# Wider store rows, and loads on a queue of their own, in a kernel that is bound by its DMA engines

## The chip, the cores and the metric

One core of one Trainium2 chip runs the kernel. The time is device microseconds of one execution; most executions of one kernel lie within 0.3% of its median, and a few of the kernel before were up to 0.8% above it (773.18 us). Every kernel that is compared by time was run in rounds beside the kernel before, on the same chip, and once with a profile; the experiments were made on three chips, so steps between them go by the ratio to the kernel before. The ratios use runs of the fast state alone.

## The reference, cut to what matters

For each of the 496 pairs (i, j) of 32 fields, a vector of 128 numbers is multiplied by the pair's own 128 x 128 matrix, and the result by another field's vector, all in float32 and for 1024 rows:

```python
v_i = inputs[:, I_IDX, :]                              # (1024, 496, 128)
v_j = inputs[:, J_IDX, :]
transformed = jnp.einsum('bpd,ped->bpe', v_i, W)       # W is (496, 128, 128)
return transformed * v_j                               # 260 MB of output
```

Output 260 MB, inputs and weights 49 MB: much traffic for the arithmetic.

## The kernel before

All inputs stay in SBUF (32 tiles of 4 KB a partition). Weights come in chunks of eight pairs, each as two half loads of 64 partitions, and are split by ScalarE and GpSimd into parts that take TensorE less time (three products that start 0.227 us apart, where the native float32 product of half a pair takes 0.858 us). ScalarE scales the first sum in PSUM, TensorE adds the correction, VectorE multiplies by the other field into an output tile, and SyncE stores the tile when its two pairs are done. SyncE issues nearly all loads too, in program order, on its one queue.

```python
OG = 2                                                       # pairs of one store
rpool = ctx.enter_context(tc.tile_pool(name="wr", bufs=3))   # raw weights
opool = ctx.enter_context(tc.tile_pool(name="o", bufs=4))    # output
...
def load_w(c, half, splits=(0, WL)):                         # WL = 8 pairs
    if c not in w_raw:
        w_raw[c] = rpool.tile([P, WL, P], F32, tag="w", name=f"w_{c}")
    for a, b in zip(splits, splits[1:]):
        nc.sync.dma_start(out=w_raw[c][half::2, a:b, :], in_=wt[c, half, :, a:b, :])
...
def second(u):                                               # u: half a pair
    ...                                                      # third matmul
    nc.vector.tensor_tensor(ots[g][:, k, s], po.pop(u), x_sb[j][:, s], ALU.mult)
    if q >= NQ - 2:
        nc.sync.dma_start(out=out[g, :, k, s], in_=ots[g][:, k, s])
    elif k == OG - 1 and h == 1:
        nc.sync.dma_start(out=out[g], in_=ots[g])
...
for u in range(2 * NQ + LAG):
    q = u // 2
    if u % (2 * WL) == 4 and (q // WL + 2) * WL < NQ:
        load_w(q // WL + 2, 1)
    if u % (2 * WL) == 12 and (q // WL + 3) * WL < NQ:
        load_w(q // WL + 3, 0)
    ...                                                      # load_x, first(u), second(u - LAG), splits
```

Of the kernel before, what the change touches and what calls it, by code (L numbers as in the profile page):

```python
# [7 lines left out]
F32 = mybir.dt.float32  # L8
# [3 lines left out]
P = 128  # L12
NF = 32
NQ = NF * (NF - 1) // 2
BT = 1024
HB = 512
WC = 2
WL = 8
OG = 2
EPS = 2.0**-12  # L20
NATIVE = 5
SHARED = 10
XDLAG = 10
LAG = 3
XLEAD = 5


def _pairs():

    return [(i, j) for i in range(NF - 2, -1, -1) for j in range(i + 1, NF)]  # L30


@with_exitstack
def kernel(
    ctx: ExitStack,
    tc: tile.TileContext,
    xt: bass.AP,
    wt: bass.AP,
    out: bass.AP,
):  # L40
















    nc = tc.nc
    pairs = _pairs()
    nchunk = NQ // WC

    xpool = ctx.enter_context(tc.tile_pool(name="x", bufs=1))
    spool = ctx.enter_context(tc.tile_pool(name="xs", bufs=2))
    rpool = ctx.enter_context(tc.tile_pool(name="wr", bufs=3))
    wpool = ctx.enter_context(tc.tile_pool(name="ws", bufs=4))
    opool = ctx.enter_context(tc.tile_pool(name="o", bufs=4))
    ppool = ctx.enter_context(tc.tile_pool(name="ps", bufs=8, space=bass.MemoryType.PSUM))

    x_sb = {}

    def load_x(f, n=1, pieces=1, eng=None):  # L70

        t = xpool.tile([P, n, BT], F32, tag=f"x{f}", name=f"x_{f}")
        s = BT // pieces
        for k in range(pieces):
            (eng or nc.sync).dma_start(out=t[:, :, k * s : (k + 1) * s], in_=xt[:, f : f + n, k * s : (k + 1) * s])
        for k in range(n):
            x_sb[f + k] = t[:, k, :]

    w_raw = {}

    def load_w(c, half, splits=(0, WL)):

        if c not in w_raw:
            w_raw[c] = rpool.tile([P, WL, P], F32, tag="w", name=f"w_{c}")
        for a, b in zip(splits, splits[1:]):
            nc.sync.dma_start(out=w_raw[c][half::2, a:b, :], in_=wt[c, half, :, a:b, :])

    w_s = {}

    def split_w(c, u):  # L90

        k = c * WC % WL
        raw = w_raw[c * WC // WL][:, k : k + WC, :].rearrange("p q e -> p (q e)")
        h, l, d = [wpool.tile([P, WC * P], F32R, tag=t, name=f"{t}_{c}") for t in ("wh", "wl", "wd")]
        nc.scalar.mul(h, raw, 1.0 - 2.0**-13)  # L95
        nc.gpsimd.tensor_tensor(l, raw, h.bitcast(F32), ALU.subtract)  # L96
        nc.gpsimd.tensor_scalar(d, h.bitcast(F32), EPS, 1.0, ALU.mult, ALU.mult)  # L97
        nc.gpsimd.tensor_tensor(d, l.bitcast(F32), d.bitcast(F32), ALU.subtract)  # L98
        w_s[c] = (h, l, d)

    x_s = {}
    later = []

    def split_x(f, a, u):

        if a == 0:
            x_s[f] = [spool.tile([P, BT], F32R, tag=t, name=f"{t}_{f}") for t in ("xh", "xl", "xd")]
        s = slice(a, a + HB)
        h, l, d = [t[:, s] for t in x_s[f]]
        nc.scalar.mul(h, x_sb[f][:, s], 1.0 - 2.0**-13)  # L110
        nc.gpsimd.tensor_tensor(l, x_sb[f][:, s], h.bitcast(F32), ALU.subtract)  # L111
        nc.gpsimd.tensor_scalar(l, l.bitcast(F32), 1.0 / EPS, 1.0, ALU.mult, ALU.mult)  # L112
        if f > NF - 2 - NATIVE - SHARED:
            later.append((min(u + XDLAG, 2 * first_q[f] + LAG - 1), d, h.bitcast(F32), l.bitcast(F32)))
        else:
            nc.gpsimd.tensor_tensor(d, h.bitcast(F32), l.bitcast(F32), ALU.subtract)  # L116

    nq0 = NATIVE * (NATIVE + 1) // 2
    c0 = nq0 // WC
    first_q = {i: q for q, (i, j) in reversed(list(enumerate(pairs)))}  # L120



    todo = []
    for c in range(c0, nchunk):
        todo.append(((c - 3) * WC + 1, max(c * WC, nq0), lambda u, c=c: split_w(c, u)))
    for i in range(NF - 2 - NATIVE, -1, -1):
        for a in range(0, BT, HB):
            todo.append((first_q[i + 1] + 1 if i < NF - 3 - NATIVE else 2, first_q[i], lambda u, i=i, a=a: split_x(i, a, u)))
    todo.sort(key=lambda t: t[1])  # L130

    load_w(0, 0, (0, 1))
    load_w(0, 1, (0, 1))
    load_w(0, 0, (1, WL))
    load_w(0, 1, (1, WL))
    load_x(NF - 2, pieces=2, eng=nc.scalar)
    load_x(NF - 1, pieces=2, eng=nc.scalar)
    load_x(NF - 3)
    load_x(NF - 4)
    load_w(1, 0)  # L140
    for f in range(NF - 5, NF - 4 - XLEAD, -1):
        load_x(f)
    load_w(1, 1)
    load_w(2, 0)


    ctx.enter_context(tc.manual_schedule())
    po, ots = {}, {}


    def first(u):
        q, h = divmod(u, 2)
        i, c = pairs[q][0], q // WC
        r = slice(q % WC * P, (q % WC + 1) * P)
        s = slice(h * HB, (h + 1) * HB)
        po[u] = ppool.tile([P, HB], F32, tag="po", name=f"po_{u}")
        if q < nq0:
            nc.tensor.matmul(po[u], w_raw[q // WL][:, q % WL, :], x_sb[i][:, s], start=True, stop=True)  # L158
        else:
            for t in (0, 1):  # L160
                nc.tensor.matmul(po[u], w_s[c][t][:, r], x_s[i][t][:, s], start=t == 0, stop=t == 1)  # L161
            nc.scalar.mul(po[u], po[u], 1.0 + EPS)  # L162

    def second(u):
        q, h = divmod(u, 2)
        i, j = pairs[q]
        r = slice(q % WC * P, (q % WC + 1) * P)
        s = slice(h * HB, (h + 1) * HB)
        if q >= nq0:
            nc.tensor.matmul(  # L170
                po[u], w_s[q // WC][2][:, r], x_s[i][2][:, s], start=False, stop=True, skip_group_check=True
            )
        g, k = divmod(q, OG)
        if k == 0 and h == 0:
            ots[g] = opool.tile([P, OG, BT], F32, tag="ot", name=f"ot_{g}")
        nc.vector.tensor_tensor(ots[g][:, k, s], po.pop(u), x_sb[j][:, s], ALU.mult)  # L176
        if q >= NQ - 2:
            nc.sync.dma_start(out=out[g, :, k, s], in_=ots[g][:, k, s])
        elif k == OG - 1 and h == 1:
            nc.sync.dma_start(out=out[g], in_=ots[g])  # L180

    for u in range(2 * NQ + LAG):
        q = u // 2
        if u % (2 * WL) == 4 and (q // WL + 2) * WL < NQ:
            load_w(q // WL + 2, 1)
        if u % (2 * WL) == 12 and (q // WL + 3) * WL < NQ:
            load_w(q // WL + 3, 0)
        if u < 2 * NQ:
            i, j = pairs[q]
            if u % 2 == 0 and j == i + 1 and 0 <= i - 2 - XLEAD:  # L190
                load_x(i - 2 - XLEAD)
            first(u)
        if u >= LAG:
            second(u - LAG)
        if u % 2 == 1:
            ready = [t for t in todo if t[0] <= q]
            if ready:
                ready[0][2](u)
                todo.remove(ready[0])
        while later and later[0][0] <= u:  # L200
            nc.vector.tensor_tensor(*later.pop(0)[1:], ALU.subtract)  # L201
    assert not todo and not later
# [27 lines left out]
```

## Time and profile before

| | before |
|---|---|
| median of 3 runs | 766.5 us |
| DMA engines, main queue's share | 98.9% |
| PE / ACT / DVE / POOL busy | 93 / 83 / 82 / 78% |
| bytes, packets | 310.12 MB, 51189 |
| VectorE waiting for a store to land | 76.3 us |

The lines themselves stand in the prediction. Read the DMA digits first: with 9 in 39 of 40 slices, work on the compute engines cannot shorten the kernel, except where it makes a transfer start earlier. In all traces of this case a row of SBUF that is contiguous in HBM shows as one packet: a store of two pairs is 128 packets of 8 KB.

### The profile page before, as it was taken

How to read it: one execution, taken by the hardware profiler on the slowest of the kernel's cores; microseconds unless marked ns; L12 is line 12 of the kernel's file. 1: busy time of each engine (PE TensorE's matmuls, PEld its weight loads, DVE VectorE, ACT ScalarE, POOL GpSimd, SP SyncE). 2: the span in 40 equal slices, each digit the busy share in tenths (PEclk: the TensorE clock that was granted, in tenths of full speed). 3: DMA queues.
4: the chain of work that ended last, by engine and by line, in shares of the span. 5: the costliest groups of instructions: out<-in, count | busy, mean ns of one | idle time of the engine just before them, and what ended most of it. 6: DMA issues, size and time to landing. Idle time of an engine off the chain costs nothing.

```text
span 766.8 us, 11879 instructions
## 1 busy us (share of the span) xinstructions
PE 715.1 (93%) x2946; PEld 547.0 (71%) x2946; DVE 631.9 (82%) x1012; ACT 634.0 (83%) x1256; POOL 594.8 (78%) x863
## 2 busy tenths in 40 slices
PE   6997999999999998999999989999999999999994
PEld 2475776677767676777776768787878777777773
DVE  3878988898877787887787878888888888888895
ACT  2186988888888898888888989998989899999893
POOL 1687998879889878878788786979787879696660
PEclk9999999999999999999999999999999999999997
DMA  9999999999999999999999999999999999999997
GB/s 341 397 419 406 414 406 385 412 397 410 415 407 409 409 393 413 410 414 413 392 424 408 401 398 405 418 414 418 418 419 421 413 408 416 410 410 411 409 399 294
DMA packets 51189, 310.12 MB, mean 404 GB/s; under 512 B 6576, under 2 KB 6704, under 8 KB 19504
## 3 DMA queue, kind: packets, MB, share of 16 engines
q1 hardware_dynamic: 50544, 308.31, 98.9%
q10 hardware_dynamic: 576, 1.05, 0.4%
q8 instruction: 24, 0.39, 0.2%
q14 instruction: 45, 0.37, 0.1%
HBM read 49.28 MB, written 260.05 MB: 403 GB/s over the span
## 4 chain that ended last, share of the span: by engine, by line
DMA 45%; PE 33%; DVE 17%; issue 2%; POOL 1%; DVEq 0%; ACT 0%; ACTq 0%; POOLq 0%
DMA out_dram<-ot 44%; PE po L161 21%; DVE ot L176 16%; PE po L170 10%; PE po L158 2%; DVE xd L201 2%; DMA x<-in_xt_dram 1%; POOL xd L116 0%; POOL xl L111 0%; POOL wl L96 0%; DVEq L176 0%; POOL wd L98 0%; POOL xl L112 0%; ACT wh L95 0%; POOL wd L97 0%
## 5 line engine op out<-in xcount | busy, mean ns | idle before, releaser
L176 DVE TENSOR_TENSOR ot<-po,x 128x512 f32<-128x512 f32 x992 | 618.6, 684 | 126.0 <-DMA out_dram<-ot 76.3
L162 ACT ACTIVATE po<-po 128x512 f32<-128x512 f32 x962 | 550.5, 583 | 103.8 <-PE po L161 56.2
L161 PE MATMUL po<-xh,wh 128*128 128x512 f32 x962 | 386.8, 402 | 26.0 <-DVE ot L176 25.0
L170 PE MATMUL po<-xd,wd 128*128 128x512 f32 x962 | 377.0, 392 | 5.4 <-DVE xd L201 4.5
L161 PE MATMUL po<-xl,wl 128*128 128x512 f32 x962 | 377.8, 393 | 3.4 <-POOL wl L96 3.4
L161 PEld LDWEIGHTS po<-xh,wh 128*128 128x128 f32 x962 | 181.1, 188 | 101.5 <-DVE ot L176 63.3
L96 POOL TENSOR_TENSOR wl<-w,wh 128x256 fp32r<-128x256 f32 x241 | 180.2, 748 | 87.0 <-ACT wh L95 77.2
L170 PEld LDWEIGHTS po<-xd,wd 128*128 128x128 f32 x962 | 181.4, 189 | 46.1 <-ACT po L162 5.2
L161 PEld LDWEIGHTS po<-xl,wl 128*128 128x128 f32 x962 | 181.4, 189 | 38.2 <-POOL wl L96 5.4
L98 POOL TENSOR_TENSOR wd<-wl,wd 128x256 fp32r<-128x256 f32 x241 | 179.9, 746 | 20.1
L97 POOL TENSOR_SCALAR wd<-wh 128x256 fp32r<-128x256 f32 x241 | 99.8, 414 | 20.3
L95 ACT ACTIVATE wh<-w 128x256 fp32r<-128x256 f32 x241 | 99.2, 412 | 3.1 <-DMA w<-in_wt_dram 3.1
L111 POOL TENSOR_TENSOR xl<-x,xh 128x512 fp32r<-128x512 f32 x52 | 67.5, 1298 | 19.7 <-ACT xh L110 19.5
L116 POOL TENSOR_TENSOR xd<-xh,xl 128x512 fp32r<-128x512 f32 x32 | 41.4, 1294 | 2.7
L110 ACT ACTIVATE xh<-x 128x512 fp32r<-128x512 f32 x52 | 32.5, 629 | 11.5 <-DMA x<-in_xt_dram 11.4
L112 POOL TENSOR_SCALAR xl<-xl 128x512 fp32r<-128x512 f32 x52 | 32.6, 628 | 4.6
L158 PE MATMUL po<-x,w 128*128 128x512 f32 x60 | 30.1, 664 | 6.0 <-DMA w<-in_wt_dram 5.0
L158 PEld LDWEIGHTS po<-x,w 128*128 128x128 f32 x60 | 12.5, 212 | 22.7 <-issue 18.8
L201 DVE TENSOR_TENSOR xd<-xh,xl 128x512 fp32r<-128x512 f32 x20 | 16.5, 826 | 0.0
L110 ACT ACT_TABLE_LOAD x1 | 1.3, 1283 | 2.7 <-issue 2.7
L217 POOL MEMSET const-float32-0.0<- 128x1 f32 x1 | 0.1, 98 | 0.2 <-issue 0.2
L217 POOL MEMSET const-bfloat16-1.0<- 128x1 bf16 x1 | 0.1, 101 | 0.0
(2 smaller groups left out, 0.2 us busy)
## 6 DMA issues: line engine op xcount, KB each, us to landing
out_dram<-ot SPq DMA_DIRECT2D x247, 1024.0 KB, 8.9
w<-in_wt_dram SPq DMA_DIRECT2D x122, 256.0 KB, 9.1
x<-in_xt_dram SPq DMA_DIRECT2D x30, 512.0 KB, 8.8
x<-in_xt_dram ACTq DMA_DIRECT2D x4, 256.0 KB, 4.0
out_dram<-ot SPq DMA_DIRECT2D x4, 256.0 KB, 7.3
w<-in_wt_dram SPq DMA_DIRECT2D x2, 224.0 KB, 5.5
w<-in_wt_dram SPq DMA_DIRECT2D x2, 32.0 KB, 3.2
```

Of the source, the lines that this page charges most:

```text
L95: nc.scalar.mul(h, raw, 1.0 - 2.0**-13)
L96: nc.gpsimd.tensor_tensor(l, raw, h.bitcast(F32), ALU.subtract)
L97: nc.gpsimd.tensor_scalar(d, h.bitcast(F32), EPS, 1.0, ALU.mult, ALU.mult)
L98: nc.gpsimd.tensor_tensor(d, l.bitcast(F32), d.bitcast(F32), ALU.subtract)
L110: nc.scalar.mul(h, x_sb[f][:, s], 1.0 - 2.0**-13)
L111: nc.gpsimd.tensor_tensor(l, x_sb[f][:, s], h.bitcast(F32), ALU.subtract)
L116: nc.gpsimd.tensor_tensor(d, h.bitcast(F32), l.bitcast(F32), ALU.subtract)
L158: nc.tensor.matmul(po[u], w_raw[q // WL][:, q % WL, :], x_sb[i][:, s], start=True, stop=True)
L161: nc.tensor.matmul(po[u], w_s[c][t][:, r], x_s[i][t][:, s], start=t == 0, stop=t == 1)
L162: nc.scalar.mul(po[u], po[u], 1.0 + EPS)
L170: nc.tensor.matmul(po[u], w_s[q // WC][2][:, r], x_s[i][2][:, s], start=False, stop=True, skip_group_check=True)
L176: nc.vector.tensor_tensor(ots[g][:, k, s], po.pop(u), x_sb[j][:, s], ALU.mult)
```

## The change

Its intent: fewer and larger packets on the engines that bind (12 KB rows), and loads that do not share a queue with the stores. Four tiles of three pairs need 16 KB a partition more; one weight tile of 4 KB is given up, since beside three weight tiles four output tiles were not expected to fit. The weights are also laid out anew in HBM, so that a chunk of eight pairs comes as one load of 512 KB and not as two halves.

```diff
-OG = 2
+OG = 3
+WB = 2
+WLEAD = 6
...
-    rpool = ctx.enter_context(tc.tile_pool(name="wr", bufs=3))
+    rpool = ctx.enter_context(tc.tile_pool(name="wr", bufs=WB))
...
-    def load_w(c, half, splits=(0, WL)):
...
+    def load_w(c, splits=(0, WL), eng=nc.scalar):
+        w_raw[c] = rpool.tile([P, WL, P], F32, tag="w", name=f"w_{c}")
         for a, b in zip(splits, splits[1:]):
-            nc.sync.dma_start(out=w_raw[c][half::2, a:b, :], in_=wt[c, half, :, a:b, :])
+            eng.dma_start(out=w_raw[c][:, a:b, :], in_=wt[c, :, a:b, :])
...
+    w_at = {}
+    for c in range(WB, -(-NQ // WL)):
+        free = (c - WB + 1) * WL if (c - WB) * WL < nq0 else 0
+        w_at[max(c * WL - 3 * WC + 1 - WLEAD, free)] = c
...
+        elif g == 0 or q >= NQ - 1 - OG:
+            if h == 1:
+                nc.sync.dma_start(out=out[g, :, k], in_=ots[g][:, k])
         elif k == OG - 1 and h == 1:
             nc.sync.dma_start(out=out[g], in_=ots[g])
...
-        if u % (2 * WL) == 4 and (q // WL + 2) * WL < NQ:
-            load_w(q // WL + 2, 1)
-        if u % (2 * WL) == 12 and (q // WL + 3) * WL < NQ:
-            load_w(q // WL + 3, 0)
...
-                load_x(i - 2 - XLEAD)
+                load_x(i - 2 - XLEAD, eng=nc.scalar)
             first(u)
+            if u % 2 == 1 and q in w_at:
+                load_w(w_at[q])
```

## The prediction

> **What bounds the kernel now.** I read the page's busy shares first, then its table of 40 slices, the DMA queues and the DMA issues, then the chain of waits and the waits of each engine, and last the DMA view in two stretches of time.
>
> From the page (engine, busy us, share of the span; then DMA busy share and GB/s by slice; then queues):
> ```profile
> span 766.8 us, 11879 instructions
> PE 715.1 (93%) x2946; PEld 547.0 (71%) x2946; DVE 631.9 (82%) x1012; ACT 634.0 (83%) x1256; POOL 594.8 (78%) x863
> ...
> DMA  9999999999999999999999999999999999999997
> ...
> DMA packets 51189, 310.12 MB, mean 404 GB/s; under 512 B 6576, under 2 KB 6704, under 8 KB 19504
> ...
> q1 hardware_dynamic: 50544, 308.31, 98.9%
> ...
> DMA 45%; PE 33%; DVE 17%; issue 2%; POOL 1%; DVEq 0%; ACT 0%; ACTq 0%; POOLq 0%
> ...
> out_dram<-ot SPq DMA_DIRECT2D x247, 1024.0 KB, 8.9
> w<-in_wt_dram SPq DMA_DIRECT2D x122, 256.0 KB, 9.1
> x<-in_xt_dram SPq DMA_DIRECT2D x30, 512.0 KB, 8.8
> x<-in_xt_dram ACTq DMA_DIRECT2D x4, 256.0 KB, 4.0
> ```
> The 16 DMA engines are the bound: one queue alone fills 98.9% of their time in every slice but the last. PE's 93% looks close, but in twenty-microsecond windows where it is never idle it does about 89 matmuls, 0.225 us each; 2886 such plus 60 native ones of 0.59 us is about 685 us, an estimate of where PE would end alone.
>
> The waits of the compute engines, then those of SyncE's queue (who <- whom: us, times, longest):
> ```profile
> POOL wl L96 <- ACT wh L95: 77.2, 94, 6.2
> DVE ot L176 <- DMA out_dram<-ot: 76.3, 93, 2.6
> PEld po L161 <- DVE ot L176: 63.3, 110, 2.4
> ```
> ```profile
> SPq L180 <- DVE ot L176: 436.0, 244, 4.0
> SPq L86 <- POOL wd L98: 26.0, 26, 1.3
> SPq L86 <- POOL wd L97: 10.2, 15, 1.2
> SPq L86 <- PE po L158: 9.7, 2, 5.7
> ```
> VectorE waits 76 us for a store to land and free its tile; PE waits behind VectorE. So compute has some 10% to spare. SyncE's 436 us is only the issuer standing ready. The loads' waits on the same queue do hold up the stores behind them, some 50 us in all, but mostly about 1 us at a time, while two or three stores are still under way.
>
> The same view in a late stretch (460 to 740 us, stores and weights only) and an early one (4 to 15 us, loads only):
> ```profile
> DMA packets 17991, 115.74 MB, mean 413 GB/s; under 512 B 2337, under 2 KB 2337, under 8 KB 5409
> ...
> q1 hardware_dynamic: 17965, 115.45, 100.3%
> ```
> ```profile
> DMA packets 1330, 4.19 MB, mean 381 GB/s; under 512 B 167, under 2 KB 178, under 8 KB 1330
> ```
> Same engines, saturated both times, and fewer GB/s with small packets: there is a cost per packet. The trace's packet records (every packet has a duration and a size) give it: medians of 84 ns for 2 KB, 159 for 4 KB, 309 for 8 KB, that is 9 ns plus 75 ns for each 2 KB, and 9 ns for a completion packet of 4 B. The means are higher, 172 ns for 4 KB and 316 for 8 KB. All packets add up to 763.9 us of 16 engines.
>
> **What the Trainium skill says.** Four places, all of "DMA: Bandwidth & Descriptors".
> "Why small descriptors are slow" gives a fixed overhead of about 3 cycles a packet. At the page's 850 MHz that is 3.5 ns; the trace agrees on the kind and shows 9 ns.
> "Where 436 GB/s comes from" puts the ceiling of the 16 ports at 435 GB/s. The slope above is 2048 B in 75 ns, 27.3 B/ns, times 16 is 437 GB/s: it agrees.
> "Issuing engines are not separate DMA queues" says that DMAs of SyncE and ScalarE run on the same 16 engines and that a second issuer saves only sequencer time. So ScalarE's queue adds no bandwidth.
> "Queues, rings and completion order" says each DMA engine goes round-robin between queues, a whole packet at a time. In the first microseconds of before, where both queues are loaded, their packets do alternate roughly one for one (88 against 61 between 5 and 6 us, in the records).
>
> **The change part by part.**
>
> Wider stores. Of 496 pairs, three at the start and two near the end go out alone (5 x 128 packets of 4 KB), the last two in halves (512 packets of 2 KB, as before), the other 489 in 163 stores of 128 rows of 12 KB. Before: 31616 packets of 8 KB x 309 / 16 = 610.6 us. After: 20864 of 12 KB; the line through the medians gives 9 + 6 x 75 = 459 ns, so 598.5 us, plus 640 x 159 / 16 = 6.4 us. Saved: 5.7 us. No packet of 12 KB to or from a tile is in the trace, so 459 is an extrapolation.
>
> Fewer DMAs. Before 251 stores + 126 weight + 34 input loads = 411, times 16 = the 6576 packets under 512 B. After 172 + 63 + 34 = 269, so 4304. 2272 packets x 9 ns / 16 = 1.3 us. The weight rows themselves stay 4 KB, twice as many to a DMA: nothing more from these.
>
> The sum is 7.0 us, all on the bound. The slices with overlap read 101%, so 6.9 us of span. The excess of means over medians (7 ns on 31616 packets, 13 ns on 11648: 24 us in all) comes mostly in clusters around loads; I let it stay at about its share of time, which takes off below 0.5 us.
>
> Loads off SyncE's queue. A load waiting for its buffer no longer blocks stores. By my count over 1 us bins of the packet records, the DMA engines lost only about 4 us to dips between 20 and 750 us, so this is worth 1 to 2 us. Start (2 us until data flows) and tail (some 5 us of landing) stay.
>
> ScalarE's price. It issues 60 weight and 24 input loads more. The four it issued before took a median of 0.45 us: 84 x 0.45 = 38 us at worst, part of it under a running activation. 634 + 38 = 672 of about 758 us, 89%. It also takes over the buffer waits of SyncE's L86 rows, some 45 us, though with two tiles and a later issue most should have passed. Against the 76 us that VectorE waits for stores, this leaves compute ahead, but by less.
>
> Two weight tiles. The load is issued 6 pairs ahead of the first split: 6 x 766.8 / 496 = 9.3 us. Its 8 packets an engine, alternating with 12 KB stores, need 8 x (159 + 459) = 4.9 us, plus about 2 us of latency: 7 us, in time by about 2 us. If one is late, ScalarE stalls, while the stores in flight (three tiles of 1.5 MB, some 3.7 us each) keep the DMA engines busy. Four tiles now hold 12 pairs instead of 8, so the compute side may fall behind by more before the DMA engines see it.
>
> Together: 766.5 - 6.9 - 1.5 = 758 us; I say 757, for some gain in stalls around loads.
>
> **The rivals.**
> 1. Two queues hide load latency. The excess of 24 us clusters where loads run: 8 KB packets in the late stretch that overlap no load packet are 4 ns over the median, those that overlap 9 or more are 18 to 22 ns over. If stores fill the holes while a load waits for HBM, half of the excess goes: 745 to 748 us. For it: the clusters. Against it: the skill's sentence that the engines are shared, and that a packet's own duration need not shrink.
> 2. Alternating costs more. If the excess is paid at each turn from store to load, one-for-one alternation makes more turns than loads in a row; doubling it gives about 780 us. For it: the same clusters. Against it: the first microseconds, where both queues hold loads and the median packet is not slower; but no trace shows loads alternating with stores.
> 3. ScalarE becomes the bound. Back to back it needs 0.565 us for each product and 0.39 us for each split: 16 and 4 in eight pairs is 10.6 us, input splits add 0.5, DMA issues up to 0.65: 11.8 us where the DMA engines need 12.2. Should issues cost 1.3 us, as loads do right behind a store on SyncE, or should buffer waits recur, it passes 12.2 and the time goes to 770 or above. Against it: those 1.3 us are a queue of issues on one sequencer, and the four of ScalarE, issued beside SyncE's, took 0.38 to 0.58 us.
> 4. The gain is hidden elsewhere: nothing moves, 765 us, if 12 KB packets take more than 459 ns (468 ns would cancel all of it).
>
> **Range and chances.** The counted saving puts it at 758 to 760; rival 1 pulls to 745, rivals 2 and 3 to 770 and more. 757, 8 in 10 between 746 and 771. Faster by over 2% means below 751.2: rival 1 in good part, 0.2. Slower by over 2% means above 781.8: rivals 2 or 3 in force, 0.07. The rest, 0.73, within.
>
> **What would show it.** Packets 51189 - 10112 - 2272 = about 38800, of them 4304 under 512 B. A 12 KB median of 459 ns. DMA digits still 9 throughout and about 409 GB/s. ScalarE's queue with about 48 MB. VectorE still waiting for stores, by less than 76 us plus what the wider tiles shift. Landing of loads near 7 us. I am wrong if the DMA digits fall in mid-span (rival 3, with long waits of ScalarE on weights), or if the packet means move by more than the row size explains (rivals 1 and 2).

## The result, and the profile after

| | before | after |
|---|---|---|
| median of 6 runs each | 766.45 us | 761.4 us |
| ratio, 95% interval | | 0.9931 (0.9912 to 0.9950) |

A ratio here and below is the mean time of one kernel's fast runs over that of the kernel before in the same rounds, so it is not quite the ratio of the medians. The gain is 0.7%, some 5.3 us. Forecast were 9.5 us, with a range of 746 to 771 us.

The page of the kernel after (busy shares, DMA by slice, packets, queues, chain, issues):

```profile
span 758.7 us, 11264 instructions
PE 708.1 (93%) x2946; PEld 551.6 (73%) x2946; DVE 633.7 (84%) x1012; ACT 625.7 (82%) x1256; POOL 595.6 (78%) x863
...
DMA  9999999999999999999999999999999999999996
...
DMA packets 38800, 310.07 MB, mean 409 GB/s; under 512 B 4304, under 2 KB 4432, under 8 KB 17872
...
q1 hardware_dynamic: 26064, 264.25, 83.1%
q10 hardware_dynamic: 12672, 45.09, 16.0%
...
DMA 40%; PE 39%; DVE 12%; POOL 5%; issue 1%; ACT 1%; DVEq 0%; ACTq 0%; POOLq 0%
...
out_dram<-ot SPq DMA_DIRECT2D x163, 1536.0 KB, 13.5
w<-in_wt_dram ACTq DMA_DIRECT2D x60, 512.0 KB, 9.0
x<-in_xt_dram ACTq DMA_DIRECT2D x24, 512.0 KB, 9.4
```

The packets are just those that were counted ahead, 38800 and 4304. The DMA engines are as full as before; the second queue (q10, ScalarE's) now carries 45 MB (the prediction said 48). The chain has moved from stores towards PE. The last number of an issue row is the landing: a weight load takes 9.0 us, where 7 had been worked out and 9.3 are to be had.

The waits of the kernel after (who <- whom: us, times, longest):

```profile
DVE ot L177 <- DMA out_dram<-ot: 46.6, 49, 1.4
ACT wh L95 <- DMA w<-in_wt_dram: 38.7, 39, 9.1
DVE ot L177 <- PE po L171: 35.1, 44, 5.1
PEld po L162 <- DVE ot L177: 33.9, 51, 1.1
```

VectorE waits less for stores, and ScalarE waits for weights 39 times: the slack of the compute side has shrunk.

The packet records, tallied by size (every packet has a duration; sums are divided by the 16 engines). "Dips" is my count of what the DMA engines lost in those 1 us bins, from 20 us to 16 us before the end, in which their share was under 0.96:

```
kernel         span    packet sum   dips   store packet (median, mean)   4 KB load (mean)
before         766.8   763.9         4.1   8 KB   309, 316 ns            172 ns
before, again  763.7   761.0         4.2   8 KB   309, 316 ns            169 ns
after          758.7   755.1         2.4   12 KB  460, 467 ns            176 ns (ScalarE's queue)
```

"Before, again" is the first experiment, and a warning: two profiles of one kernel differ by 3 us. Against the second the span falls by 5.0 us, like the timed runs; against the first by 8.1.

### The profile page after: what moved, and what is told of

The parts are those of the page before. It is cut to its first block, busy times and chain, and to the rows that moved or that the text cites. A ratio compares the mean times of both kernels' runs of the same rounds, so it can differ in the third digit from the quotient of the medians.

```text
span 758.7 us, 11264 instructions
## 1 busy us (share of the span) xinstructions
PE 708.1 (93%) x2946; PEld 551.6 (73%) x2946; DVE 633.7 (84%) x1012; ACT 625.7 (82%) x1256; POOL 595.6 (78%) x863
## 2 busy tenths in 40 slices
DMA packets 38800, 310.07 MB, mean 409 GB/s; under 512 B 4304, under 2 KB 4432, under 8 KB 17872
## 4 chain that ended last, share of the span: by engine, by line
DMA 40%; PE 39%; DVE 12%; POOL 5%; issue 1%; ACT 1%; DVEq 0%; ACTq 0%; POOLq 0%
DMA out_dram<-ot 34%; PE po L162 24%; DVE ot L177 12%; PE po L171 12%; DMA w<-in_wt_dram 6%; PE po L159 4%; POOL xl L111 1%; POOL xd L116 1%; POOL wl L96 1%; POOL xl L112 1%; POOL wd L98 1%; ACT po L163 0%; DMA x<-in_xt_dram 0%; DVE xd L203 0%; POOL wd L97 0%
## 5 line engine op out<-in xcount | busy, mean ns | idle before, releaser
L163 ACT ACTIVATE po<-po 128x512 f32<-128x512 f32 x962 | 540.7, 582 | 58.6 <-PE po L162 24.4
L162 PE MATMUL po<-xh,wh 128*128 128x512 f32 x962 | 382.6, 398 | 13.6 <-DVE ot L177 12.9
L95 ACT ACTIVATE wh<-w 128x256 fp32r<-128x256 f32 x241 | 99.8, 415 | 42.3 <-DMA w<-in_wt_dram 38.7
L111 POOL TENSOR_TENSOR xl<-x,xh 128x512 fp32r<-128x512 f32 x52 | 69.2, 1331 | 18.6 <-ACT xh L110 18.3
L159 PE MATMUL po<-x,w 128*128 128x512 f32 x60 | 28.3, 634 | 4.5 <-DMA x<-in_xt_dram 4.5
## 6 DMA issues: line engine op xcount, KB each, us to landing
out_dram<-ot SPq DMA_DIRECT2D x163, 1536.0 KB, 13.5
```

The lines of the kernel that those rows point to most:

```text
L95: nc.scalar.mul(h, raw, 1.0 - 2.0**-13)
L111: nc.gpsimd.tensor_tensor(l, x_sb[f][:, s], h.bitcast(F32), ALU.subtract)
L159: nc.tensor.matmul(po[u], w_raw[q // WL][:, q % WL, :], x_sb[i][:, s], start=True, stop=True)
L162: nc.tensor.matmul(po[u], w_s[c][t][:, r], x_s[i][t][:, s], start=t == 0, stop=t == 1)
L163: nc.scalar.mul(po[u], po[u], 1.0 + EPS)
```

## The experiments

Twelve more runs were made, eleven of them of an edited kernel. Each time is a median, each ratio one to the kernel before in the same rounds.

**1. The kernel before, profiled once more** (label before_again, no edit).

> A second profile of the kernel before, to see how far two executions of one kernel differ in the part of the packet time that lies over the medians. All theories: the same 51189 packets, medians 84, 159 and 309 ns, a packet sum within 3 us of 763.9. If that sum differs by more than 3 us, the 3 us by which this excess fell from before to after (24.6 to 21.6 us) prove nothing.

Measured: 765.6 us, 51189 packets, the same medians, packet sum 761.0 us (above). The part over the medians was 21.9 us, where the first profile had 24.7 and the kernel after 21.7. In experiments 3 and 7, with the loads on ScalarE's queue too, it was about 24 and 19 us. So this part did not change beyond what two profiles of one kernel differ by; rivals 1 and 2 of the prediction, which needed a change of 12 us or more, both fall.

**2. Wide stores alone** (label wide_o3). The kernel before with

```diff
-OG = 2
+OG = 3
-    opool = ctx.enter_context(tc.tile_pool(name="o", bufs=4))
+    opool = ctx.enter_context(tc.tile_pool(name="o", bufs=3))
```

and the edge stores of the change.

> Wide stores alone: loads as before on SyncE's queue with three weight tiles, stores of three pairs, from three output tiles since four do not fit. Theory of the packet count: 9952 fewer packets of data or so and 79 fewer store issues, 6 us off: 760 us, ratio 0.992. Rival (the gain of the whole change is from the queue of its own): 766 us. Rival (the tiles give less cover): slower than before, with the DMA digits under 9.

Measured: 783.49 us, ratio 1.0208 (1.0186 to 1.0231). Slower by 2%, with the same bytes and 11379 packets fewer. In the packet records the dips rose to 13.7 us, and the part over the medians to 36.3 us. One such dip, in windows of wide stores alone (columns: stretch, its length, busy time of PE, PEld, DVE, ACT and POOL, clock, DMA share, GB/s), and SyncE's queue over the same time (start, length, issue):

```profile
466.00:470.00 4.00, 2.62 (x12) 1.84 (x11) 1.93 (x5) 2.35 (x5) 3.66 (x7) 1.00 1.00 402
470.00:472.00 2.00, 2.00 (x10) 1.64 (x9) 2.00 (x4) 1.68 (x4) 0.15 (x2) 1.00 0.71 299
472.00:474.00 2.00, 2.00 (x10) 1.47 (x9) 1.42 (x3) 1.80 (x4) 1.76 (x3) 1.00 0.60 254
474.00:478.00 4.00, 4.00 (x19) 3.05 (x17) 3.41 (x7) 3.68 (x9) 2.38 (x4) 1.00 0.97 354
```

```profile
466.65 6.08 SPq L183 DMA_DIRECT2D out_dram<-ot  x2
472.78 0.93 SPq L86 DMA_DIRECT2D w<-in_wt_dram  x1
```

The share of the DMA engines falls to 0.71 and 0.60 between 470 and 474 us. SyncE was holding a store that waited for VectorE (5.3 us, its longest wait in this stretch); VectorE in turn had waited 2.1 us for one of the three tiles to come free. When that store goes, a weight load follows at once: it had been standing behind it. All fourteen dips of this profile that I looked up end in this way, with a store and a load right behind it. That alone proves little, since 113 of the 156 stores between 20 and 740 us have a load right behind them. But at all fourteen GpSimd had read the old weights of the load's buffer for the last time 3.3 to 14.6 us before, so the load had been ready. Five of the six dips looked up in the kernel before end in the same way, where 123 of 239 stores have a load right behind them; here is the one at 457 us, first the windows and then the queue:

```profile
452.00:456.00 4.00, 3.16 (x14) 2.32 (x13) 2.63 (x5) 2.80 (x6) 3.67 (x7) 1.00 1.03 422
456.00:458.00 2.00, 2.00 (x10) 1.36 (x8) 1.40 (x4) 1.67 (x4) 1.83 (x4) 1.00 0.76 315
```

```profile
456.82 0.33 SPq L180 DMA_DIRECT2D out_dram<-ot  x1
457.24 1.16 SPq L86 DMA_DIRECT2D w<-in_wt_dram  x1
```

The prediction had this the wrong way round: not stores behind a load that waits for its buffer, but loads behind a store that waits for VectorE. SyncE's waits say the same: it waited for VectorE at 161 of the 163 wide stores of this run, and of the 122 right behind a load, 120 started more than 0.2 us after the load's issue had ended, so the load had not held them.

```profile
SPq L183 <- DVE ot L176: 494.6, 161, 7.1
```

**3. Loads alone** (label loads_act_og2; against the kernel before it has the other queue, whole loads and two weight tiles, all three at once). The kernel after with

```diff
-OG = 3
+OG = 2
-        elif g == 0 or q >= NQ - 1 - OG:
-            if h == 1:
-                nc.sync.dma_start(out=out[g, :, k], in_=ots[g][:, k])
```

> Loads alone: ScalarE's queue, two weight tiles, whole 512 KB loads, but stores of two pairs from four tiles as before. Theory of the packet count: only 62 fewer load issues, 0.6 us, and 1 to 2 us less blocking: 764 to 766 us, ratio 0.997 to 1.0. Rival (two queues hide load latency): 755 to 760 us. Rival (ScalarE and late weights are the price): 770 us or more, with the DMA digits under 9.

Measured: 764.18 us, ratio 0.9963 (0.9941 to 0.9985). Half of the whole gain, 2.8 us, with nearly the packets of before (50179). The dips fell to 2.1 us. How much of this is the queue and how much the 62 loads fewer was not run apart; at 8 KB rows the queue alone stays untested.

**4. The row size by itself** (labels rows4k and rows2k). The kernel after; one store is still one issue of 1.5 MB, but the output tensor is laid out so that it falls into shorter rows (the 2 KB form splits each pair in two as well). This also spreads a store over several places of HBM, which the test cannot part from the row size.

```diff
-            nc.sync.dma_start(out=out[g], in_=ots[g])
+            nc.sync.dma_start(out=out[g].rearrange("k p b -> p k b"), in_=ots[g])
```

> The kernel after, with the output laid out so that each store, still one issue of 1.5 MB, falls into 4 KB rows. Theory of the packet cost: 62592 packets of 159 ns in place of 20864 of 460 ns is 22 us more of 16 engines, so 783 us, ratio to before 1.021. Rival (the rate does not depend on the row at these sizes): 761 us.

> The kernel after with stores of the same size cut into 2 KB rows. 62592 packets more than with 4 KB rows. If a packet really costs the 9 ns of the recorded durations: 35 us over the 4 KB run, 803 us. If, as the 4 KB run suggests (packet sum up by 20 us, span by 7), records overlap and a packet costs 3 to 4.6 ns: 12 to 18 us over the 4 KB run, 779 to 786 us, with a DMA share that reads 1.04 or more.

Measured: 767.52 us for 4 KB rows, ratio 1.0009 (0.9983 to 1.0034), and 798.82 us for 2 KB (the three fast runs), ratio 1.0406 (1.0372 to 1.0440). Neither time was forecast: the first lies between the theory and the rival, the second between the two figures given, nearer to 803. The two pages (span, packets):

```profile
span 765.6 us, 11264 instructions
...
DMA packets 80528, 310.07 MB, mean 405 GB/s; under 512 B 4304, under 2 KB 4432, under 8 KB 80464
```

```profile
span 794.9 us, 11264 instructions
...
DMA packets 143760, 310.07 MB, mean 390 GB/s; under 512 B 4304, under 2 KB 4432, under 8 KB 143696
```

From 12 to 4 KB there are 41728 packets more. The packet sum rises from 755.1 to 775.2 us, as 9 ns a packet has it, yet the span only from 758.7 to 765.6. By the timed ratios the step costs (1.0009 - 0.9931) x 766.45 = 6.0 us, that is 6.0 x 16 / 41728 = 2.3 ns a packet (about 1.4 to 3.2 by the two intervals). From 4 to 2 KB it is (1.0406 - 1.0009) x 766.45 = 30.4 us over 62592 packets, 7.8 ns each. In the bins without dips the DMA share reads 1.010 after, 1.023 with 4 KB rows and 1.041 with 2 KB: recorded durations overlap those of their neighbours, more so the shorter the packets. The sum of durations is therefore not the time that the engines need; for large rows most of the fixed 9 ns is hidden. Two other things changed with the 4 KB rows: loads landed in 7.8 us in place of 9.0, and the dips came to 0.7 us in place of 2.4, which may mask up to 1.7 us of what packets cost (then 3 ns each). Why so little is hidden at 2 KB stays open.

**5. A tile less, with the queues apart** (label after_o3). The kernel after with `bufs=3` for the output.

> The kernel after with three output tiles in place of four. Theory of cover (wide stores need four tiles; three hold 9 pairs with only two stores in flight, and the slowest DMA engine or a late load then stops the rest): 770 us or more, ratio to before above 1.005, with dips in the DMA share as in the run of wide stores alone. Rival (that run lost its time because loads blocked SyncE's queue, not for want of a tile): 761 to 764 us.

Measured: 761.28 us, ratio 0.9928 (0.9903 to 0.9953), the same as the kernel after. My theory of cover fell and its rival held: three tiles are enough when loads have their own queue. The wait of VectorE for stores rose to 67.7 us and the dips to 5.9, and it cost no time that the runs can tell; stores now landed in 9.1 us in place of 13.5.

**6. All loads back on SyncE** (label loads_sp_og3). The kernel after with

```diff
-    def load_w(c, splits=(0, WL), eng=nc.scalar):
+    def load_w(c, splits=(0, WL), eng=nc.sync):
-                load_x(i - 2 - XLEAD, eng=nc.scalar)
+                load_x(i - 2 - XLEAD)
```

> The kernel after with its loads issued by SyncE on the store queue, at the same places in the program. Theory (the own queue is what makes two weight tiles possible): a load lands after up to three stores of 1.5 MB ahead of it, about 12 us, while the first split follows 9.3 us after its issue, so ScalarE waits for weights at each load: 770 us or more. Rival (the queue does not matter, as the bytes are the same): 761 to 764 us.

Measured: 778.99 us, ratio 1.0159 (1.0129 to 1.0188), 2.3% over the kernel after with nothing changed but the queue. Its waits, and its chain by engine on the page:

```profile
DVE ot L177 <- PE po L171: 73.4, 63, 7.0
ACT wh L95 <- DMA w<-in_wt_dram: 67.0, 24, 12.5
```

```profile
PE 61%; DMA 23%; POOL 9%; DVE 2%; issue 2%; ACT 2%; ACTq 0%; DVEq 0%; POOLq 0%
```

ScalarE waits up to 12.5 us for weights and VectorE behind it; compute has become the chain. A load landed 10.3 us after its issue, and in the stretch of SyncE's queue that I read (200 to 260 us) each weight load was issued right behind a store that had waited for VectorE. In the whole run none of the 73 stores right behind a load started less than 0.8 us after it, so here too it was the loads that were held, by stores or, 12 of 59 of the weights, by a buffer that had only just come free. With experiment 5 this settles what experiment 2 left open: wide stores lose with loads on their queue, from three tiles or four, and gain with loads on the other, from three tiles or four.

**7. Two-pair stores from six tiles** (label og2_o6): experiment 3 with `bufs=6`, so the same SBUF and pairs as the kernel after.

> Loads as in the kernel after, stores of two pairs in 8 KB rows as before, but from six tiles: the same 48 KB and 12 pairs of cover as after. If row size gives the gain at 3 to 4.6 ns a packet: 2 to 3 us over the kernel after, ratio to before 0.995 to 0.997, the same as with four tiles of two pairs. Rival (cover gives the gain, not the rows): ratio 0.993, as after.

Measured: 763.22 us, ratio 0.9946 (0.9923 to 0.9968). Between the kernel after and loads alone, and not to be told from either, so rows and cover are not told apart for certain. By the middle values, this and experiment 3 leave for the wide rows a step of 0.15 to 0.32%, 1 to 2.5 us.

**8. Weights asked for earlier** (label wlead8): `WLEAD = 8` in the kernel after.

> The kernel after with each weight load issued 8 pairs ahead of its first split in place of 6, 12 us in place of 9. Theory (the DMA engines are the bound and late weights are covered by stores in flight): ScalarE's wait for weights falls from 39 us to under 15, the time stays within 0.3% of the kernel after, ratio to before 0.991 to 0.996. Rival (late weights take back part of the gain): 756 to 758 us, ratio 0.988 or less.

Measured: 763.88 us, ratio 0.9948 (0.9919 to 0.9977): not faster, as the theory had it. ScalarE's wait for weights fell to 15.5 us (forecast: under 15). Its largest waits now:

```profile
ACT wh L95 <- POOL wl L96: 51.1, 27, 4.3
ACT po L163 <- PE po L162: 19.6, 29, 2.3
```

Waiting for weights has turned into waiting for GpSimd, which must finish with the old weights first. With two weight tiles, asking 8 pairs ahead in place of 6 brought nothing: half of the weight loads were now issued within 0.5 us of the moment that their buffer came free.

**9. Compute with little to store** (label store_third; two of three pairs are never stored).

```diff
-            nc.sync.dma_start(out=out[g], in_=ots[g])
+            nc.sync.dma_start(out=out[g, :, k], in_=ots[g][:, k])
```

> Wrong result on purpose: of every three pairs only the last is stored, so that the DMA engines have little to do and the compute engines set the time. Theory (compute has about 7 to 10% to spare, and the loads issued by ScalarE cost it little): 685 to 715 us. Rival (ScalarE with its issues and waits is nearly the bound): 740 us or more.

Measured: 728.65 us in two runs, between the two forecasts. Its page:

```profile
PE 691.9 (95%) x2946; PEld 552.3 (76%) x2946; DVE 683.0 (94%) x1012; ACT 625.6 (86%) x1256; POOL 594.7 (82%) x863
...
DMA  9775465655554454463545545344444453545545
...
PE 81%; POOL 12%; DVE 3%; DMA 2%; issue 1%; ACTq 0%; DVEq 0%; ACT 0%; POOLq 0%; SPq 0%
```

The DMA engines are half idle, PE and GpSimd make the chain. So the compute side ends about 4% before the kernel after, not 10%. ScalarE is not the bound.

**10. A step further** (labels og4_o3, wl16_o3). Stores of four pairs in 16 KB rows from three tiles (`OG = 4`, `bufs=3`, edges moved by one pair); and three tiles of three pairs with weights 16 pairs at a time, 10 ahead (`WL = 16`, `WLEAD = 10`, the first loads reordered).

> One step further: stores of four pairs in 16 KB rows from three tiles (the same 48 KB). 4992 packets fewer and 41 issues fewer. At the 2.3 to 3 ns a packet that 4 KB against 12 KB rows showed: under 1.5 us off, ratio to before 0.990 to 0.994, not to be told from the kernel after. At 9 ns: 3 us, ratio 0.989. Rival (cover of two stores in flight is too little): over 0.995.

> Since three output tiles did as well as four, their 12 KB go to weights: 16 pairs to a tile, 8 KB rows and 1 MB loads, issued 10 pairs ahead. 3900 packets fewer and 31 issues fewer: 1 to 2 us off the kernel with three tiles, ratio to before 0.989 to 0.993. Rival (a 1 MB load in one go delays stores or comes late): 0.995 or more.

Measured: 768.61 us, ratio 1.0019 (0.9978 to 1.0059), and 774.19 us, ratio 1.0096 (1.0062 to 1.0131). Both give the gain back. With 16 KB rows ScalarE waits 72.7 us for weights, and DMA dips come to 18.4 us. With 1 MB weight loads there is little such waiting; instead the 8 KB load packets took 412 ns in the mean at a median of 309, and the packet sum rose to 770.0 us. What slows them I did not find. Both profiles are of the slowest of six runs (774.59 and 778.31 us), so they overstate what the medians lost. Of both expectations it was the rival's time that came; what the first rival named, too little cover, is not what the trace shows. No version beats the kernel after; that with three tiles equals it with 12 KB a partition to spare.

## Why the prediction was right or wrong

The direction was right and the range held; the size was nearly twice too large. By its own steps:

- **The bound.** Right: the DMA engines were the bound before and are after (digits of 9; experiment 9 frees them and the time falls). "Some 10% to spare" for compute was mis-sized: 4 to 5%, by 728.65 against 761.4 and 766.9 us. The estimate of 685 us for PE left out its waits, 22.0 us of them for GpSimd (experiment 9).
- **Wider stores, 5.7 us.** The term that was mis-sized. Counts and durations were right (20864 packets, a median of 460 for the 459 ns forecast; all packets at their medians come to 5.8 us less, where 7.0 had been counted). "All on the bound" was wrong: durations overlap, and between 12 and 4 KB rows a packet costs 2.3 ns of time, not 9. For 10112 packets that is 10112 x 2.3 / 16 = 1.5 us; experiments 3 and 7 leave 1 to 2.5.
- **Fewer DMAs, 1.3 us.** Count right (4304); what it is worth was not measured by itself.
- **Loads off SyncE's queue, 1 to 2 us.** Measured 2.8 us (1.2 to 4.5 by the interval), with whole loads and two tiles in it. That the number came near is luck, for the mechanism was told backwards: the loads stood behind waiting stores. The 50 us for which loads are said to hold up stores were misread: 51 of the 55 waits of loads listed for SyncE end within the load's own issue, and from the fifth chunk on each of the 116 weight loads was issued at least 1.0 us after its buffer had come free. Of the 129 full stores right behind a load, 119 started more than 0.2 us after the load's issue had ended, so at most ten were held by a load. And I took this part for an addition to the other. It is the condition of the other: wide stores with loads on the one queue lose 1.6 to 2.1% (experiments 2 and 6).
- **ScalarE's price, up to 38 us of issues.** Overstated, and rightly called harmless: an issue took 0.33 us, and ScalarE was busy for 626 us.
- **Two weight tiles, in time by 2 us.** Wrong by those 2 us: landing took 9.0 us. In the records a load's first packet starts 2.3 us after the issue, its last 5.4 us later, and the landing is reported 1.3 us after that (medians of 34 loads): the 4.9 us of moving were near, the 2 us of latency too few. One for one is not how it looks close up: in the half microsecond in which most load packets start, about 20 of them start beside 10 of stores (means of 21 loads). The 88 against 61 packets of the prediction are counts of one microsecond (2 to 6 us: 475 against 250) and show no order. Nor does the section "Queues, rings and completion order" of "DMA: Bandwidth & Descriptors" speak of rows: its packet is a group of descriptors, typically 9 to 17. The stall (38.7 us of ScalarE) was covered, as foreseen; asking earlier gained nothing.
- **Rivals.** 1 and 2 fell with the unchanged part over the medians (21.7 us, against 21.9 and 24.7). 3 did not come true here; late weights did bind with loads on SyncE and with 16 KB rows. 4 in its form (12 KB packets slow enough to cancel the gain) fell with the median of 460 ns; its sum was off, since 7.0 us would be cancelled by 459 + 7.0 x 16000 / 20864 = 464 ns and not by 468. But its drift, a saving that isn't time, is what happened to the wide stores.

The 48 MB for ScalarE's queue were added wrongly: 60 + 24 loads of 0.52 MB and the 1.05 MB of before are 45.

The 5.3 us are thus about half loads and half rows, with cover perhaps a part of the second half. The two were added from separate runs with intervals of 1 to 2 us each, so the halves are rough.

## What to carry to other kernels

Where the DMA engines are the bound, ask of every queue not only what its transfers wait for, but what stands behind them: here a store that waited for compute held back loads that were ready, and a second issuer cured that though it added no bandwidth. A sum of packet durations overstated what larger rows save; change the row size alone and time it before giving SBUF to it. With compute only 4 to 5% behind the DMA engines, neither of the two further steps gained anything.

## What the Trainium skill lacked or had wrong

- "DMA: Bandwidth & Descriptors", section "Issuing engines are not separate DMA queues", says that a second issuer saves only the sequencer's time, which is usually small. Bandwidth agrees (409 GB/s after, 404 before). But an in-order queue of issues holds ready loads behind a waiting store: moving the same loads between queues changed 761.4 to 778.99 us, with wide stores and two weight tiles. "Perfetto Trace Analysis", section "DMA Optimizations", does name separate issuers for inputs and outputs, without this reason or a number.
- "DMA: Bandwidth & Descriptors", section "Why small descriptors are slow": about 3 cycles a packet; an estimate of 3.5 ns, if they are cycles of the 850 MHz that the page gives for the fabric. The runs show no one figure: 9 ns in the records, 2.3 ns of time between 12 and 4 KB rows, 7.8 ns between 4 and 2 KB.
- "Perfetto Trace Analysis", section "DMA Optimizations", gives batching from 2 KB to 4 or 8 KB as its example of what can help dramatically, and speaks of the size of a DMA, not of its rows. With stores of 1.5 MB throughout, the runs show a gain of 4.0% from 2 to 4 KB rows and of 0.8% from 4 to 12 KB (ratios 1.0406, 1.0009, 0.9931).
- On neither page: that the packet durations which a trace records overlap, so that their sum is more than the engines' time. With 2 KB rows the DMA share reads 1.041 of it.
- On neither page: how far apart the 16 engines of one DMA finish. With four wide tiles the last of a store's 16 engines reported 3.8 us after the fifteenth on average, with three tiles 0.9 us, at the same time of the whole (761.4 and 761.3 us); with four tiles and 4 KB rows it was 0.5 us, so the number of tiles alone does not set it.
